# Four tokens to a partition, one factor for the first batch, and a tail that is planned backwards

## The chip, the cores and the metric

The kernel runs on one core of one Trainium2 chip. The metric is the device time in microseconds from start to end of one launch. A core has five engines that run side by side, each in the order of its own instructions: TensorE (PE, matrix products), VectorE (DVE), ScalarE (ACT), GpSimd (POOL) and SyncE (SP, here only an issuer of transfers). Each waits on semaphores for what it needs of the others.

## The reference

Four layers of a graph network over 32 batches of 512 tokens with 128 features; `adj` is one 512 x 512 matrix for all. Each layer adds its result to x.

```python
h = relu(layernorm(x));  x = x + L0(h, adj)       # GCN
h = relu(layernorm(x));  x = x + L1(h, adj)       # gated graph network, 5 steps
h = relu(layernorm(x));  x = x + L2(h, adj)       # graph attention, softmax over neighbours, elu
h = relu(layernorm(x));  x = x + L3(h, adj)       # graph attention without elu

# L0
A = adj + I;  d = A.sum(-1) ** -0.5
out = (d[:, None] * A * d[None, :]) @ h @ W.T + b
# L1, five times (in_matrix and out_matrix are both adj)
m = adj @ h
z = sigmoid([m, m] @ w3.T + h @ u3.T + ...);  r = sigmoid([m, m] @ w4.T + h @ u3.T + ...)
hv = tanh([m, m] @ w5.T + (r * h) @ u5.T + ...);  h = (1 - z) * h + z * hv
# L2, L3
g = h @ W;  e = leaky_relu(g @ a_src + (g @ a_dst).T), only where there is an edge
out = softmax(e) @ g
```

## The kernel before

The kernel doesn't write its instructions in program order. It collects operations, each with an engine, an estimated cost, a due time and what it reads and writes. Then a planner simulates the engines with those costs and emits the instructions in the order that it found. The buffers are pools: a value takes a free one when its first operation starts, and gives it back after the last.

```python
class Plan:
    def run(self):
        for o in reversed(self.ops):
            o.tail = o.cost + o.delay + max((q.tail for q in o.then), default=0)
        ...
        best = min(self.ends, key=lambda end: self.attempt(uses, *end))
        self.attempt(uses, *best)
        for o in self.order:
            o.emit()

    def attempt(self, uses, last, hurry):
        for o in self.ops:
            o.soon = min(o.due, last - o.tail * hurry)     # the priority of an operation
        # ... list scheduling: of the ready operations of an engine for which buffers
        #     are free, the one with the smallest o.soon starts

# pools (cut):  8 PSUM banks, 13 x, 2 "e" (scores, [128, 4, 512] f32), 4 "off", ...
# 16 pairs (last, hurry) are tried
```

Loads. Token c * 128 + p lies on partition p, so a partition gets four pieces of 512 bytes of x; of adj it gets one row of 2 KB per piece c.

```python
nc.sync.dma_start(v.t, x[b].rearrange("(c p) d -> p c d", p=P))              # L259, each batch
q.dma_start(adj_sb.t[:, c, :], adj[c * P:(c + 1) * P, :])                    # L264, on ACT and SP in turn
w0 = load("w0", ...)                                                         # L237, then b0, w4, w3, w5, u3, u5
```

The start. adj is turned on TensorE (L295), its degrees are summed (two pieces on ScalarE, two on VectorE, L303), and one power on GpSimd makes `dinv` (L306). Batch 0 is normalized on VectorE with its own power `rstd` (L402), and then multiplied by `dinv`. Its product with adj takes adj + I on the diagonal blocks (`diag`, L314).

```python
op("POOL", 1.0, ..., pow(deg, -0.5) -> dinv)                                 # L306
for m in range(C):
    op("DVE", 0.16, ..., diag[m] = block(adjT, m) + ident)                   # L314
...
norm(b, y, -802)                     # bn_stats, bn_aggr, pow on POOL (L402), (x - mean) * rstd (L423)
op("DVE", 0.16, ..., y = max(y, 0) * dinv)                                   # L596, four times

def product(h, due):                                                         # L559
    for c in range(C):
        for lo, hi in ((0, c), (c, c + 1), (c + 1, C)):
            if lo < hi:
                right = diag.t[:, c, :] if lo == c else adjT.t[:, c, lo * P:hi * P]
                nc.tensor.matmul(..., h.t[:, c, :], right, ...)
```

The GCN of the later batches and the steps of the gated network form their products with adj by seven half products for a pair of batches (L520), of which four take prepared sums of adj's quarters ("made"). There are two such sets, one of adj and one of the normalized adj ("an").

The tail. The attention of the last four batches ("near") takes the path through TensorE in place of transfers: centre and relu on VectorE, turn, heads, score rows spread by TensorE, scores on VectorE, and a mix that starts with each score block.

```python
def center_relu(b, y, due):
    for c in range(C):
        op("DVE", 0.21, ..., bn_stats(st[c], x[c]))                          # L431
        op("DVE", 0.07, ..., bn_aggr(mv[c], st[c]))                          # L432
        op("DVE", 0.16, ..., y[c] = max(x[c] - mean[c], 0))                  # L433
    op("DVE", 0.1, ..., ve = var + EPS)                                      # L436
    op("POOL", 1.0, ..., rstd = ve ** -0.5)                                  # L437

# gat, near:  turn y (L452), copy (L730), heads (L743), exp of three columns (L748),
#   factor g (L751), scale (L756), spread the row (L772), then for each block j:
#   e[j] = max(row, column) * mask             on VectorE, 128 x 512         # L785
#   four products of e[j] with h               on TensorE, 128 x 129         # L794
#   reciprocal (L808), then L2: v (L810), exp (L824), sums (L825, L827);  L3: x += p * rden (L816), output (L838)
# the other batches: mix at L805, gates of the gated network at L653, L654, L660, L667, L668
```

Of the kernel before, what the change touches and what calls it, by code (L numbers as in the profile page):

```python
# [15 lines left out]
P = 128  # L16
# [7 lines left out]
FAR0, FAR1 = 2, 4  # L24
RUN_UP = 8
# [14 lines left out]
class Op:  # L40
    def __init__(self, engine, cost, due, emit, delay):
        self.engine, self.cost, self.due, self.emit, self.delay = engine, cost, due, emit, delay
        self.waits, self.then, self.vals = 0, [], []


class Plan:
# [5 lines left out]
    def __init__(self, buffers, ends):  # L52
        self.buffers, self.ends, self.ops = buffers, ends, []

# [28 lines left out]

    def run(self):

        for o in reversed(self.ops):
            o.tail = o.cost + o.delay + max((q.tail for q in o.then), default=0)
            o.first = o.waits
        uses = {v: v.uses for o in self.ops for v in o.vals}
        best = min(self.ends, key=lambda end: self.attempt(uses, *end))  # L90
        self.attempt(uses, *best)
        assert self.end < math.inf, "the order has come to a stop"
        for o in self.order:
            o.emit()

    def attempt(self, uses, last, hurry):
        for v, n in uses.items():
            v.uses = n
            if v.kind:
                v.t = None  # L100
        for o in self.ops:
            o.waits = o.first

            o.soon = min(o.due, last - o.tail * hurry)
# [7 lines left out]
        now, count = 0.0, 0  # L112
# [6 lines left out]
        def start(e):  # L119
            if busy[e]:  # L120
                return
            kept = []
            while ready[e]:
                key = heapq.heappop(ready[e])
                o = self.ops[key[1]]
                opens = [v for v in o.vals if v.kind and v.t is None]
                short = [v for v in opens if len(free[v.kind]) < sum(u.kind == v.kind for u in opens)]
                if not short:
                    for v in opens:
                        v.t = free[v.kind].pop()  # L130
                    busy[e] = True
                    o.at = now
                    order.append(o)
                    post(now + o.cost, 0, o)
                    post(now + o.cost + o.delay, 1, o)
                    break
                kept.append(key)
            for key in kept:
                heapq.heappush(ready[e], key)

# [9 lines left out]
        while events:  # L150
            now, _, kind, o = heapq.heappop(events)
            if kind == 0:
                busy[o.engine] = False
                settle(o, True)
            else:
                done += 1
                settle(o, False)
                for v in o.vals:
                    v.uses -= 1
                    if not v.uses and v.kind:  # L160
                        free[v.kind].append(v.t)
            for e in ready:
                start(e)
# [5 lines left out]
def gnn_stack(ctx: ExitStack, tc: tile.TileContext, a: dict, out: bass.AP):  # L169
# [3 lines left out]
    C = N // P  # L173

# [8 lines left out]
    def flat(t):  # L183
# [25 lines left out]
        "e": tiles(2, [P, C, N], "e"),  # L209
# [6 lines left out]
        "off": tiles(4, SMALL, "off"),  # L216
        "rden": tiles(3, SMALL, "rden"),
    }, [(last, hurry) for last in (170, 173, 176, 179) for hurry in (0.06, 0.08, 0.1, 0.12)])
# [15 lines left out]
    def load(name, shape, src, due, queue="SP", cost=0.45, delay=3.6):  # L234
        v = fixed(shape, name)
        q = {"SP": nc.sync, "POOL": nc.gpsimd, "AQ": nc.scalar}[queue]
        op(queue if queue != "AQ" else "ACT", cost, due, lambda: q.dma_start(v.t, src), w=[v], delay=delay)  # L237
        return v
# [17 lines left out]
    for b in range(B):  # L256
        v = Val("x", C)
        op("SP", 0.5, -1002 if b == 0 else max(-995 + b, STEPS * b - 20) if b >= 8 else -995 + b,
           lambda v=v, b=b: nc.sync.dma_start(v.t, x[b].rearrange("(c p) d -> p c d", p=P)), w=[v], delay=3.5 if b == 0 else 3 if b > 3 else 4)  # L259
        xs.append(v)  # L260
    adj_sb = Val("e", C)
    for c in range(C):
        e, q = (("ACT", nc.scalar), ("SP", nc.sync))[c % 2]
        op(e, 0.45, -1001, lambda c=c, q=q: q.dma_start(adj_sb.t[:, c, :], adj[c * P:(c + 1) * P, :]),  # L264
           w=[adj_sb[c]], delay=3 if c == 0 else 4.2)
    w0 = load("w0", [P, D], a["L0_gnn_W"], -994.5)
# [4 lines left out]
    for k in ("w4", "w3", "w5", "u3", "u5"):  # L271
        src = a[f"L1_gnn_{k}_w"]
        raw[k] = load(k, [P, src.shape[1]], src, -993.3)
# [15 lines left out]
    for c in range(C):  # L289
# [3 lines left out]
        def turn_adj(c=c, p=p):  # L293
            for m in range(C):
                nc.tensor.transpose(p.t[:, m, :], adj_sb.t[:, c, m * P:(m + 1) * P], ident.t)  # L295
        op("PE", C * TURN, -800, turn_adj, r=[adj_sb[c], ident], w=[p])
        op("ACT", A, -800, lambda c=c, p=p: nc.scalar.copy(adjT.t[:, :, c * P:(c + 1) * P], p.t), r=[p], w=[adjT[c]])
        if c < 2:
# [3 lines left out]
        else:  # L302
            op("DVE", 0.66, -801, lambda c=c: nc.vector.reduce_sum(deg.t[:, c:c + 1], adj_sb.t[:, c, :], axis=mybir.AxisListType.X),  # L303
               r=[adj_sb[c]], w=[deg[c]])
    op("DVE", 0.1, -801, lambda: nc.vector.tensor_scalar_add(deg.t, deg.t, 1.0), w=[deg])
    op("POOL", 1.0, -1000, lambda: nc.gpsimd.tensor_tensor(dinv.t, deg.t, mhalf.t, ALU.pow), r=[deg, mhalf], w=[dinv])  # L306

# [5 lines left out]
    for m in range(C):  # L313
        op("DVE", 0.16, -799.5, lambda m=m: nc.vector.tensor_add(diag.t[:, m, :], block(adjT.t, m), ident.t),  # L314
           r=[adjT[m], ident], w=[diag[m]])

    def right_factors(mT, due):


        made = fixed([P, 4, 2, 2 * P], "made", 4)  # L320
# [4 lines left out]
        f |= {k: (lambda i=i: made.t[:, i], made[i]) for i, k in enumerate((2, 1, 4, 6))}  # L325
# [20 lines left out]
    def transposed(due, *group, then=()):  # L346

        p = Val("bank", len(group))
        t = fixed([P, len(group), P], "wT")
        for i, (parts, _) in enumerate(group):  # L350
# [3 lines left out]
            op("PE", len(parts) * MM1, due, turns, r=[ident, minus, *then] + [q[0] for q in parts], w=[p[i]])  # L354
# [13 lines left out]
    w0T = transposed(-750, (one(w0), 1), then=turned)  # L368
    gates = transposed(-700, (halves("w4"), 1), (one(raw["u3"]), 1), (halves("w3") + halves("w4", minus), 1), (halves("w5"), 1), then=turned)
    u5T = transposed(-690, (one(raw["u5"]), 0.5), then=turned)  # L370
# [21 lines left out]
    def norm_stats(b, due):  # L392
        xb, st, mv, ve, rstd = xs[b], Val("st", C), Val("mv"), Val("ve"), Val("rstd")
# [8 lines left out]
        op("POOL", 1.0, due, lambda: nc.gpsimd.tensor_tensor(rstd.t, ve.t, mhalf.t, ALU.pow), r=[ve, mhalf], w=[rstd])  # L402
        return mv, rstd

    def norm_relu(b, y, due, times=None):

        xb, off = xs[b], Val("off")
        mv, rstd = norm_stats(b, due)
# [9 lines left out]
    def norm(b, y, due):  # L418

        xb = xs[b]  # L420
        mv, rstd = norm_stats(b, due)
        for c in range(C):
            op("DVE", 0.16, due, lambda c=c: nc.vector.tensor_scalar(  # L423
                y.t[:, c, :], xb.t[:, c, :], mv.t[:, c, 0:1], rstd.t[:, c:c + 1], op0=ALU.subtract, op1=ALU.mult),
               r=[xb[c], mv, rstd], w=[y[c]])

    def center_relu(b, y, due):

        xb, st, mv, ve, rstd = xs[b], Val("st", C), Val("mv", C), Val("ve"), Val("rstd")
        for c in range(C):  # L430
            op("DVE", 0.21, due, lambda c=c: nc.vector.bn_stats(st.t[:, c, :], xb.t[:, c, :]), r=[xb[c]], w=[st[c]])  # L431
            op("DVE", 0.07, due, lambda c=c: nc.vector.bn_aggr(mv.t[:, c, :], st.t[:, c, :]), r=[st[c]], w=[mv[c]])  # L432
            op("DVE", 0.16, due, lambda c=c: nc.vector.tensor_scalar(  # L433
                y.t[:, c, :], xb.t[:, c, :], mv.t[:, c, 0:1], 0.0, op0=ALU.subtract, op1=ALU.max),
               r=[xb[c], mv[c]], w=[y[c]])
# [115 lines left out]
    def product(h, due):  # L551

        p, m = Val("bank"), Val("m")
        for c in range(C):
            def times(c=c):
                for lo, hi in ((0, c), (c, c + 1), (c + 1, C)):
                    if lo < hi:
                        right = diag.t[:, c, :] if lo == c else adjT.t[:, c, lo * P:hi * P]
                        nc.tensor.matmul(flat(p.t)[:, lo * P:hi * P], h.t[:, c, :], right, start=c == lo == 0, stop=c == C - 1,  # L559
                                         skip_group_check=True)  # L560
            op("PE", MM, due, times, r=[h[c], adjT[c], diag[c]], w=[p, m])
# [3 lines left out]
    def normalized(begun):  # L565
# [18 lines left out]
        return anT, right_factors(anT, 0)  # L584
# [4 lines left out]
    def gcn(pair, due):  # L589
        first, ys = pair[0] < 4, []  # L590
        for i, b in enumerate(pair):
            y = Val("y", C) if first else Val("pair", 2)
            if b == 0:
                norm(b, y, -802)
                for c in range(C):
                    op("DVE", 0.16, -800, lambda c=c, y=y: nc.vector.tensor_scalar(  # L596
                        y.t[:, c, :], y.t[:, c, :], 0.0, dinv.t[:, c:c + 1], op0=ALU.max, op1=ALU.mult), r=[dinv], w=[y[c]])
            else:
                norm_relu(b, y, -798 if b == 1 else due + i, dinv if first else None)
# [4 lines left out]
        ms = [product(y, due + i) for i, y in enumerate(ys)] if first else products(*ys, factors["an"], due + 1)  # L604
# [117 lines left out]
    def gat(b, l, due):  # L722
# [113 lines left out]
        elif near:  # L836
            for a in range(2):
                op("SP", 0.45, due + 4, lambda a=a: nc.sync.dma_start(  # L838
                    out[b].rearrange("(c p) d -> p c d", p=P)[:, 2 * a:2 * a + 2], xb.t[:, 2 * a:2 * a + 2]),
                   r=[xb[2 * a], xb[2 * a + 1]])  # L840
        else:
            op("SP", 0.95, due + 4, lambda: nc.sync.dma_start(out[b].rearrange("(c p) d -> p c d", p=P), xb.t), r=[xb])
# [63 lines left out]
```

## Time and profile before

| what | value |
|---|---|
| time, median of 3 runs | 1633.63 us (1631.4 to 1633.82) |
| span of the profiled run | 1631.2 us |
| mean granted TensorE clock | 0.999 |
| TensorE, VectorE, ScalarE, GpSimd busy | 99%, 85%, 44%, 9% |
| transfers | 374176 packets, 157.72 MB, 38.5% of 16 engines' time in the main queue |

How to read it: a matrix product of 32-bit floats shows as two records[...]; a turn by the transpose instruction shows as one. The records of TensorE overlap, so a mean duration is longer than the distance from one start to the next, and the pieces of the chain of waits give the better rate. A row of the timeline has the start, the length, the engine, the line, the operation, the tiles and, in brackets, how long the engine was idle before it and what released it.

### The profile page before, as it was taken

To read this page: it belongs to the slowest core of one execution; us is meant where nothing else is said; L and a number is where in the kernel's file an instruction comes from. 1 tells how busy PE (TensorE), PEld (TensorE's weight loads), DVE (VectorE), ACT (ScalarE), POOL (GpSimd) and SP (SyncE) were. 2 spreads that over 40 slices of the span, in tenths; PEclk is the share of its full clock that TensorE was granted. 3 is DMA by queue.
4 is the path that set the end of the run, shared out by engine and by line. 5 is a ranking of instruction groups with operands and counts; after the bars stand their busy time and mean duration, and the time that the engine had idled before them with its cause. 6 is when DMAs were issued, how large, how long until landed. Compare 5 with 4: busy or idle time off the path is not lost.

```text
span 1631.2 us, 23929 instructions
## 1 busy us (share of the span) xinstructions
PE 1617.3 (99%) x7330; PEld 1169.2 (72%) x7330; DVE 1386.3 (85%) x3989; ACT 716.1 (44%) x1593; POOL 143.2 (9%) x136
## 2 busy tenths in 40 slices
PE   9999999999999999999999999999999999999998
PEld 7666666776776777777776766767677777676777
DVE  8968688898978898888898888888887888777888
ACT  5653443535335344444535345353443533434343
POOL 2200000010001100000111001110000000000001
PEclk9999999999999999999999999999999999999999
DMA  4134353534436344353433535344362323434010
GB/s 130 33 71 104 81 120 91 124 98 106 115 82 147 82 117 104 91 135 84 121 101 96 137 79 134 88 106 118 82 146 73 98 72 84 123 91 110 27 40 27
DMA packets 374176, 157.72 MB, mean 97 GB/s; under 512 B 201664, under 2 KB 355616, under 8 KB 374048
## 3 DMA queue, kind: packets, MB, share of 16 engines
q1 hardware_dynamic: 373760, 155.67, 38.5%
q8 instruction: 58, 0.95, 0.2%
q14 instruction: 70, 0.57, 0.1%
q10 hardware_dynamic: 288, 0.52, 0.1%
HBM read 86.25 MB, written 69.84 MB: 96 GB/s over the span
## 4 chain that ended last, share of the span: by engine, by line
PE 95%; DVE 3%; ACT 1%; DMA 0%; POOL 0%; issue 0%; DVEq 0%; POOLq 0%; ACTq 0%
PE bank L520 35%; PE bank L805 12%; PE bank L653 8%; PE bank L654 8%; PE bank L667 8%; PE bank L660 8%; PE bank L668 8%; PE bank L743 3%; PE bank L612 2%; PE bank L559 1%; PE bank L794 1%; DVE e L785 1%; PE bank L452 1%; POOL rstd L402 0%; DMA w<-in_L_gnn_w_w_dram 0%
## 5 line engine op out<-in xcount | busy, mean ns | idle before, releaser
L520 PE MATMUL bank<-made,S 128*128 128x256 f32 x1128 | 269.5, 380 | 1.2 <-ACT half L525 0.9
L402 POOL TENSOR_TENSOR rstd<-ve,mhalf 128x4 f32<-128x4 f32 x120 | 132.8, 1108 | 1397.5 <-DVE ve L400 1130.6
L520 PEld LDWEIGHTS bank<-made,S 128*128 128x128 f32 x1128 | 217.2, 196 | 40.4 <-issue 17.2
L525 ACT COPY half<-bank 128x256 f32<-128x256 f32 x282 | 104.4, 370 | 258.7 <-PE bank L520 255.7
L805 PEld LDWEIGHTS bank<-h_gat,e 128*128 128x128 f32 x1792 | 207.9, 192 | 13.0 <-issue 11.2
L805 PE MATMUL bank<-h_gat,e 128*128 128x129 f32 x1792 | 208.6, 275 | 0.0
L656 ACT ACTIVATE r<-bank,gate_bw 128x512 f32<-128x512 f32 x160 | 109.6, 685 | 213.5 <-PE bank L654 190.2
L672 DVE TENSOR_TENSOR hv<-hv,hT 128x512 f32<-128x512 f32 x160 | 109.3, 683 | 85.3 <-ACT hv L670 84.9
L658 DVE SCALAR_TENSOR_TENSOR rh<-r,hT 128x512 f32<-128x512 f32 x160 | 110.0, 687 | 67.4 <-ACT r L656 66.5
L653 PE MATMUL bank<-m,wT 128*128 128x512 f32 x320 | 163.7, 593 | 0.0
L667 PE MATMUL bank<-m,wT 128*128 128x512 f32 x320 | 163.4, 592 | 0.0
L654 PE MATMUL bank<-hT,wT 128*128 128x512 f32 x320 | 163.4, 592 | 0.0
L668 PE MATMUL bank<-rh,wT 128*128 128x512 f32 x320 | 163.4, 592 | 0.0
L660 PE MATMUL bank<-m,wT 128*128 128x512 f32 x320 | 163.3, 592 | 0.0
L670 ACT ACTIVATE hv<-bank,gate_bw 128x512 f32<-128x512 f32 x160 | 109.5, 684 | 118.9 <-PE bank L668 117.6
L785 DVE SCALAR_TENSOR_TENSOR e<-row,h_gat,maskT 128x512 f32<-128x512 f32 x224 | 161.4, 740 | 0.0
L520 PE MATMUL bank<-adjT,h 128*128 128x256 f32 x640 | 159.5, 380 | 0.5 <-ACT h L687 0.5
L520 PEld LDWEIGHTS bank<-adjT,h 128*128 128x128 f32 x640 | 123.3, 196 | 25.2 <-issue 13.4
L533 DVE TENSOR_TENSOR m<-half,bank 128x256 f32<-128x256 f32 x282 | 115.9, 412 | 24.3 <-ACT half L525 12.0
L662 ACT ACTIVATE z<-bank,gate_bw 128x512 f32<-128x512 f32 x160 | 109.6, 685 | 51.5 <-PE bank L660 49.8
L395 DVE BATCH_NORM_STATS2 st<-x 128x6 f32<-128x128 f32 x480 | 115.4, 279 | 4.7 <-DMA x<-in_x_dram 4.4
L654 PEld LDWEIGHTS bank<-hT,wT 128*128 128x128 f32 x320 | 60.8, 190 | 76.5 <-issue 75.1
(137 smaller groups left out, 2278.8 us busy)
## 6 DMA issues: line engine op xcount, KB each, us to landing
far<-sq SPq DMA_DIRECT2D x920, 64.0 KB
h<-far SPq DMA_DIRECT2D x240, 128.0 KB
gT<-far SPq DMA_DIRECT2D x56, 256.0 KB
row<-line SPq DMA_DIRECT2D x56, 256.0 KB
x<-in_x_dram SPq DMA_DIRECT2D x32, 256.0 KB
h<-far SPq DMA_DIRECT2D x28, 256.0 KB
out_dram<-x SPq DMA_DIRECT2D x28, 256.0 KB
hT<-far SPq DMA_DIRECT2D x104, 64.0 KB
```

Source lines behind the costliest of these rows:

```text
L395: op("DVE", 0.21, due, lambda c=c: nc.vector.bn_stats(st.t[:, c, :], xb.t[:, c, :]), r=[xb[c]], w=[st[c]])
L402: op("POOL", 1.0, due, lambda: nc.gpsimd.tensor_tensor(rstd.t, ve.t, mhalf.t, ALU.pow), r=[ve, mhalf], w=[rstd])
L520: nc.tensor.matmul(low(r), u[:, l, :], factors[k][0]()[:, l, :], start=fresh and l == 0, stop=l == 1, skip_group_check=not fresh)
L533: op("DVE", HV, due - 5, lambda: nc.vector.tensor_add(out(), u.t, low(t)), r=[u, t], w=[o])
L653: nc.tensor.matmul(flat(gate.t), gates.t[:, 0, :], flat(m.t), start=True, stop=False)
L654: nc.tensor.matmul(flat(gate.t), gates.t[:, 1, :], flat(hT.t), start=False, stop=True)
L658: op("DVE", V, due - 5, lambda: nc.vector.scalar_tensor_tensor(flat(rh.t), flat(r.t), 1.0, flat(hT.t), op0=ALU.add, op1=ALU.mult), r=[r, h ...
L660: op("PE", MM, due + 0.3, lambda: nc.tensor.matmul(flat(gate.t), gates.t[:, 2, :], flat(m.t), start=False, stop=True, skip_group_check=Tru ...
L667: nc.tensor.matmul(flat(cand.t), gates.t[:, 3, :], flat(m.t), start=True, stop=False)
L668: nc.tensor.matmul(flat(cand.t), u5T.t[:, 0, :], flat(rh.t), start=False, stop=True)
L785: op("DVE", 0.68, due + 3, lambda j=j: nc.vector.scalar_tensor_tensor(e.t[:, j, :], rows(row.t), h.t[:, j, D + 1:D + 2], mask(j), op0=ALU. ...
L805: nc.tensor.matmul(pt()[:, c, :D + 1], e.t[:, j, i * P:(i + 1) * P], h.t[:, j, :D + 1], start=(j == 0), stop=(j == C - 1))
```

## The change

- Layout: token p * 4 + c lies on partition p, so a partition's part of x and of the result is one piece of 2 KB (1 KB for the outputs of the last four batches, which go in two halves). adj is loaded and turned in the same order of tokens.
- Batch 0: relu(x - mean) is multiplied by one factor ((deg + 1)(var + eps)) ** -0.5, whose power is taken in two pieces (three columns, then one). Its product adds h times the identity instead of reading `diag`. Weights are loaded in another order, and some are turned later.
- The last four batches: the relu after centring moves from VectorE to ScalarE.
- A third score buffer "e"; the second set of made factors is kept in one of the three until the last GCN pair is done.
- The planner: it starts from three pairs (last, hurry), and from each goes up to five times through the plan backwards, from the end, to find how late each operation may start; operations after 1350 us of the plan take that as their priority. After 1420 us it may put an idle transpose on TensorE where 0.9 us of the last 3.4 would be without work.
- Estimated delays of the first loads are set anew.

The diff, shortened: "..." marks cuts, and some bodies are told in a line.

```diff
-        best = min(self.ends, key=lambda end: self.attempt(uses, *end))
-        self.attempt(uses, *best)
+        for last, hurry in self.ends:
+            for again in range(6):
+                if again:
+                    late = self.put_off()
+                for o in self.ops:
+                    if not again:
+                        o.soon = min(o.due, last - o.tail * hurry)
+                    else:
+                        o.soon = late[o] / self.SLOT if o.at > self.near_end else o.due
+                self.attempt()
+    def put_off(self):
+        # list scheduling from the end: an operation is ready when all that need it are placed,
+        # and of the ready ones that which ended last in the plan so far comes first
...
+            if e == "PE" and left and not busy[e] and now > self.idle_from and free["bank"]:
+                keep_going()
...
-        "e": tiles(2, [P, C, N], "e"),
+        "e": tiles(3, [P, C, N], "e"),
-        "off": tiles(4, SMALL, "off"),
+        "off": tiles(6, SMALL, "off"),
-    }, [(last, hurry) for last in (170, 173, 176, 179) for hurry in (0.06, 0.08, 0.1, 0.12)])
+    }, [(179, 0.06), (175, 0.06), (177, 0.12)], 1350,
+        IDLE_FROM, lambda v: nc.tensor.transpose(v.t[:, 0, :], ident.t, ident.t))
...
-           lambda v=v, b=b: nc.sync.dma_start(v.t, x[b].rearrange("(c p) d -> p c d", p=P)), ...)
+           lambda v=v, b=b: nc.sync.dma_start(v.t, x[b].rearrange("(p c) d -> p c d", c=C)), ...)
-        op(e, 0.45, -1001, lambda c=c, q=q: q.dma_start(adj_sb.t[:, c, :], adj[c * P:(c + 1) * P, :]), ...)
+        op(e, 0.45, -1001, lambda c=c, q=q: q.dma_start(adj_sb.t[:, c, :], adj.rearrange("(p c) n -> c p n", c=C)[c]), ...)
-                nc.tensor.transpose(p.t[:, m, :], adj_sb.t[:, c, m * P:(m + 1) * P], ident.t)
+                nc.tensor.transpose(p.t[:, m, :], adj_sb.t[:, c].rearrange("p (n m) -> p m n", m=C)[:, m], ident.t)
...
-        made = fixed([P, 4, 2, 2 * P], "made", 4)
+        made = Val("e", 4) if passing else fixed([P, C, N], "made", 4)      # passing for "an"
...
-    w0T = transposed(-750, (one(w0), 1), then=turned)
+    w0T = transposed(-9.2, (one(w0), 1), then=turned)
+    # of the gates' weights u3 and w5 are due at -9.5, w4 and w3 stay at -700; u5 at -9.4
...
+    def norm_first(b, y):
+        for parts in ((0, 2, 1), (3,)):
+            op("DVE", 0.8, ..., deg of the last part;  f = (deg + 1) * ve)
+            op("POOL", 1.0, ..., f = f ** -0.5)
+            op("DVE", 0.1, ..., off = -mean * f)
+        op("DVE", 0.2, ..., y[0] = max(x[0] - mean, 0));  op("DVE", 0.2, ..., y[0] *= f[0])
+        for c in range(1, C):
+            op("ACT", 0.385, ..., y[c] = relu(f[c] * x[c] + off[c]))
...
     def center_relu(b, y, due):
-            op("DVE", 0.16, ..., y[c] = max(x[c] - mean[c], 0))
+        for a in range(2):
+            op("DVE", 0.22, ..., bn_aggr of two pieces, off = -mean)
+            op("ACT", 0.385, ..., y[c] = relu(x[c] + off[c]))               # twice
...
     def product(h, due, by_diag):
+                if by_diag:
+                    terms = [(0, c, row[:, :c * P]), (c, c + 1, diag.t[:, c, :]), (c + 1, C, row[:, (c + 1) * P:])]
+                else:
+                    terms = [(0, C, row), (c, c + 1, ident.t)]              # batch 0
...
-                    out[b].rearrange("(c p) d -> p c d", p=P)[:, 2 * a:2 * a + 2], ...)
+                    out[b].rearrange("(p c) d -> p c d", c=C)[:, 2 * a:2 * a + 2], ...)
```

## The prediction

> **What bounds the kernel now.** I read the page first (busy time and the chain that ended last), then the windows by stage, and then the timeline of the first 12 us and the chain of the last 50 us. From the page:
>
> ```profile
> span 1631.2 us, 23929 instructions
> PE 1617.3 (99%) x7330; PEld 1169.2 (72%) x7330; DVE 1386.3 (85%) x3989; ACT 716.1 (44%) x1593; POOL 143.2 (9%) x136
> ...
> PE 95%; DVE 3%; ACT 1%; DMA 0%; POOL 0%; issue 0%; DVEq 0%; POOLq 0%; ACTq 0%
> ```
>
> TensorE is busy 99% of the span and is 95% of the chain. The change removes no product, so its whole field is the time in which TensorE does not work at its rate. How much is that? Busy time overlaps and flatters, so I use start-to-start times from the chain: 0.429 us for a record of 512 columns ("0.86 PE bank L653 x2"), 0.2165 for 256 ("3.46 PE bank L520 x16"), 0.1117 for 129 or 131, 0.11 for 128. Counts from the groups: 2632 x 0.2165 = 570, 1600 x 0.429 = 686, 2048 x 0.1117 = 229, 512 x 0.1117 = 57, the rest about 63. Sum 1605 us, the warm-up at the start left out. The span less the 4.35 us until the first piece of adj has landed, and less the 5.3 us behind the last product (last sums on VectorE and the output's landing), is 1621.5. So about 16.5 us are lost, 1% of the span, and a change of this kind cannot reach 2% (32 us). Where they lie (windows; columns: stretch, its length, then busy time and count of PE, PEld, DVE, ACT, POOL, then clock, DMA share, GB/s):
>
> ```profile
> 0.00:10.00 10.00, 7.75 (x44) 7.13 (x45) 5.03 (x24) 5.33 (x12) 2.86 (x9) 1.00 0.84 250
> ...
> 400.00:800.00 400.00, 399.51 (x1781) 287.00 (x1781) 348.24 (x997) 178.22 (x390) 36.76 (x33) 1.00 0.43 107
> ...
> 1580.00:1600.00 20.00, 19.43 (x167) 18.69 (x166) 19.34 (x76) 9.00 (x32) 2.47 (x3) 1.00 0.05 14
> 1600.00:1610.00 10.00, 9.57 (x82) 8.94 (x81) 10.00 (x35) 3.92 (x12) 1.53 (x2) 1.00 0.01 2
> 1610.00:1620.00 10.00, 7.96 (x56) 7.49 (x55) 8.74 (x36) 4.09 (x17) 1.01 (x1) 0.83 0.09 26
> 1620.00:1631.20 11.20, 6.77 (x61) 6.58 (x59) 6.40 (x21) 0.69 (x3) 0.00 (x0) 1.00 0.25 72
> ```
>
> The middle is full. The tail is not, and there VectorE is at 97 to 100% while ScalarE is at 40 to 45%; from 1610 the clock falls to 0.83. The chain of the tail shows the same:
>
> ```profile
> 1612.79 0.20 DVE off L751 x3
> 1613.00 1.33 DVE e L785 x2
> 1614.33 0.04 issue
> 1614.38 1.12 PE bank L772 x4
> 1615.49 2.80 PE bank L794 x16
> ...
> 1620.51 5.38 PE bank L794 x48
> ```
>
> The chain runs on VectorE nearly without a break from 1585.2 to 1614.3. After that TensorE is slow: 16 records in 2.80 us and 4 in 1.12, where the row of 48 gives 0.112 each (1.79 and 0.44). That is 1.7 us lost to the clock alone. The start, from the timeline:
>
> ```profile
> 6.03 1.69 PE L295 MATMUL bank<-ident,e 128*128 128x128 f32 x12 [0.35 <-DMA e<-in_adj_dram]
> 7.56 0.39 PE L353 MATMUL bank<-ident,w 128*128 128x128 f32 x2
> 8.79 1.16 PE L353 MATMUL bank<-ident,w 128*128 128x128 f32 x8 [0.84 <-DMA w<-in_L_gnn_w_w_dram]
> 8.91 1.59 POOL L306 TENSOR_TENSOR dinv<-deg,mhalf 128x4 f32<-128x4 f32 x1 [1.39 <-DVE deg L305]
> 10.54 0.88 DVE L596 TENSOR_SCALAR y<-y,dinv 128x128 f32<-128x128 f32 x4 [0.31 <-POOL dinv L306]
> 11.13 0.39 PE L559 MATMUL bank<-v,y 128*128 128x128 f32 x2
> ```
>
> The first product waits for two powers on GpSimd in a row (rstd, then dinv); TensorE fills the time with turned weights and waits for those too.
>
> **What the Trainium skill says.** "TensorE: Matmul & The Clock Gate", section "What's actually happening": the clock is passed or halved by how busy TensorE was in a window of about 3.4 us. The trace agrees in kind: the slow records come after waits of 0.40 us at 1609.6 and 1.93 us at 1613.6. "VectorE: DVE Perf Modes", section on the TRN2 errata: each operation from SBUF pays a fixed time beside its elements, on VectorE and ScalarE. The trace agrees: a 128x512 score takes 742 ns and a 128x128 centring still 276 alone (about 195 back to back). So moving a small operation from one engine to the other moves its whole fixed cost. "DMA: Bandwidth & Descriptors", section "Why small descriptors are slow (HBM only)": a fixed cost per packet. In this trace the queues stand at 300 to 400 GB/s from 3 to 10 us, with 512-byte and 2 KB packets mixed; how much the 512-byte ones cost there no row tells.
>
> **The change part by part.**
>
> *Layout.* An x load goes from 512 packets of 512 bytes to 128 of 2 KB, an output alike (1 KB in the last four batches). adj's rows were 2 KB before. All 32 loads and outputs but the first four lie under the full middle: worth 0 there. Only the start can feel it, where x0, x1 and 1 MB of adj share the queues.
>
> *Batch 0 by one factor.* Relu commutes with the positive factor, so rstd and dinv become one power of (deg+1)(var+eps). From the instruction order of the changed kernel with the durations above: adj is all turned at 7.6 as before; VectorE has the stats of x0 by 6.35, one centring and one sum of degrees by about 7.3; GpSimd's power of three columns (1.0 to 1.1 us) ends at about 8.6; the first y is ready at about 8.8, against 10.8. Product 0 now has 4 x (512 + 128) columns in two passes, 4 x 1.08 = 4.3 us against 3.5, since it adds the identity instead of waiting for the diagonal sums. Before it TensorE turns only 12 weight records (w4 and w3, now loaded earlier, so the wait of 0.84 goes); the other 10 (1.1 us) come after. So y1 is wanted at 8.9 + 4.3 + 1.1 = 14.3 us, against 14.76 before, with the same work done. Gain about 0.4 us; 2.3 us earlier in the first product is mostly paid back in the longer product and the weights that move behind it.
>
> *Relu of the last four batches on ScalarE.* Per attention 4 centrings (4 x 0.195) leave VectorE and 2 small negations (2 x 0.075) come: 0.6 us less, eight times. ScalarE has room (45% busy). It costs latency: four relus at about 0.39 instead of 0.2.
>
> *Third score buffer.* It is the place of the second set of made factors, which ends with the last GCN pair; so it is free exactly for the tail, and two attentions need no longer wait for each other's e.
>
> *Planned backwards.* The order is what matters. In the old order 40.1 us of TensorE work (counted, at the rates above) lie behind the last gate product, which ends at 1579.9; the last product ends at 1625.9. So 46.0 us for 40.1: 5.9 lost. In the new order 46.4 us of work lie behind it (28 + 108 + 44 + 24 + 32 instructions there against 24 + 112 + 16 + 24 + 32): attention products of earlier batches are held back as filling. VectorE's work behind the last new state is 39.2 us against 37.5, with a head of some 4 us before it: 43, against 46.4 + 2.5 for TensorE and the last sums. So VectorE has 5.7 us of slack where it had none (37.5 with a head of 5 from 1579.9 to 1585, 42.5 against 42.6). No filler product (the idle transpose) was placed at all, so the plan sees no 3.4 us stretch with 0.9 us of idling after 1420. I estimate 1.5 of the 5.9 us remain: 4.4 gained, the clock's 1.7 within it. From 1400 to 1580 about 3.6 us are lost before; I let the change win 1.5.
>
> Sum: 0.4 + 4.4 + 1.5 = 6.3 us. 1633.6 - 6.3 = 1627.3, said as 1627.5.
>
> **The rivals.** First, everything fits: the tail keeps no loss, the wider packets bring x0 in half a microsecond earlier. For it: the counted slack on VectorE. That is 5.9 + 3 + 1.5, about 10 us, 1623. Second, the new order is right only by the plan's own costs, and each engine runs in order: a late small operation stops TensorE. For it: powers on GpSimd took 1.0 to 1.6 us in the trace where the plan writes 1.0, and VectorE runs attentions of four batches interleaved with little between them; relus on ScalarE make the last batch's chain longer by about 0.8 us in each of two attentions. That would give back 3 to 5 us: 1630 to 1632. Third, the change of priorities moves the middle too (the order differs nearly from the first row), and a shuttle through memory then lands late. For it: seven waits of TensorE for a copied half product, 3.2 us in all. Against it: DMA share 0.43 and nothing of the middle's chain on DMA. It could cost 2 to 6 us: up to 1634.
>
> **Range and chances.** The gain has a ceiling of about 12 us (16.5 less what a start and an end always cost) and a floor a little above zero if the second or third rival holds. I take 1622 to 1632.5. A change by 2% either way is outside anything the trace offers.
>
> **What would show it.** Start: the first batch-0 product near 8.9 us and batch 1's near 14.3. Tail: the chain on TensorE, not VectorE, from the last gate on; clock 1.00 in every window; TensorE behind the last gate losing under 2 us; the stretch from there to the end about as long as before (some 51 us) while the last gate comes 4 to 6 us earlier. Wrong it would be if VectorE still ended the waits of the tail, if the clock still fell, or if the middle lost what the tail won.

## The result, and the profile after

| | before | after |
|---|---|---|
| time, median | 1633.57 us (6 runs, 1631.4 to 1633.82) | 1624.25 us (6 runs, 1623.91 to 1625.03) |
| ratio after / before | | 0.9946, 95% interval 0.9933 to 0.9959 |
| span of the profiled run | 1631.2 us | 1623.2 us |
| packets | 374176 | 350113 |

The change takes 9.3 us off the median; by the ratio in the table that is 0.54%. The page of the changed kernel, its top and its chain:

```profile
span 1623.2 us, 24004 instructions
PE 1614.7 (99%) x7326; PEld 1169.0 (72%) x7326; DVE 1378.4 (85%) x3971; ACT 724.6 (45%) x1628; POOL 146.1 (9%) x137
...
PE 94%; DVE 3%; DMA 1%; ACT 0%; POOL 0%; issue 0%; SPq 0%; DVEq 0%; ACTq 0%; POOLq 0%
```

The top of the page hardly moved: TensorE had 99% and has 99%. The gain can only be seen by stage. The windows of the changed kernel (columns as in the table of before: PE, PEld, DVE, ACT, POOL with counts, clock, DMA share, GB/s):

```profile
0.00:10.00 10.00, 7.78 (x36) 7.12 (x37) 4.21 (x22) 4.93 (x11) 2.41 (x10) 1.00 0.69 223
...
400.00:800.00 400.00, 400.00 (x1796) 288.85 (x1795) 348.01 (x993) 174.81 (x387) 34.75 (x31) 1.00 0.43 107
...
1450.00:1500.00 50.00, 50.00 (x234) 35.88 (x233) 41.33 (x108) 21.01 (x46) 2.36 (x3) 1.00 0.43 106
...
1580.00:1600.00 20.00, 20.00 (x180) 19.87 (x179) 19.79 (x71) 11.27 (x43) 2.01 (x2) 1.00 0.13 48
1600.00:1610.00 10.00, 9.46 (x85) 9.27 (x84) 9.70 (x45) 5.75 (x20) 2.01 (x2) 1.00 0.04 14
1610.00:1623.20 13.20, 9.28 (x82) 8.92 (x80) 9.11 (x28) 2.71 (x11) 0.00 (x0) 1.00 0.24 81
```

From 1400 to 1600 TensorE now has no gap (in the kernel before it was busy 48.80 of the 50 us from 1450 to 1500), and the clock stays at 1.00 to the end. VectorE is as busy in the tail as before (19.79 of 20), but it no longer sets the pace: ahead of the last sums it has one stretch of 5.7 us left in the chain, from 1601.9 to 1607.6.

```profile
1598.13 3.57 PE bank L905 x32
1601.70 0.23 PE bank L883 x2
1601.94 0.01 issue
1601.95 0.17 DVE rden L919
...
1606.92 0.66 DVE e L896
1607.59 0.04 issue
1607.63 1.16 PE bank L905 x8
...
1613.96 5.38 PE bank L905 x48
1619.33 0.02 issue
1619.36 0.17 DVE rden L919
...
1620.03 0.52 DVE x L927 x2
```

The start went the other way. Timeline of the start (start, length, engine, line, operation, count, idle before); L342 is the warm-up, products of zeros that only keep TensorE busy until adj is there:

```profile
1.05 3.78 PE L342 MATMUL bank<-hv 128*128 128x128 f32 x16 [1.05 <-DVE hv L335]
...
5.53 0.63 ACT L390 ACTIVATE r<-e 128x512 f32<-128x512 f32 x1 [2.18 <-DMA e<-in_adj_dram]
...
5.65 1.10 PE L385 MATMUL bank<-ident,e 128*128 128x128 f32 x4 [0.81 <-DMA e<-in_adj_dram]
7.10 2.72 PE L385 MATMUL bank<-ident,e 128*128 128x128 f32 x12 [0.35 <-DMA e<-in_adj_dram]
9.66 1.06 PE L440 MATMUL bank<-ident,w 128*128 128x128 f32 x8
10.55 0.61 PE L440 MATMUL bank<-minus,w 128*128 128x128 f32 x4
11.00 1.02 PE L673 MATMUL bank<-adjT,y 128*128 128x512 f32 x2
```

adj's first piece landed at 5.53 us (4.36 before; here and below this is when ScalarE's first sum of it starts), and the 12 turns after it took 2.56 us from their first start to the next operation (1.53 before). So the first product came at 11.00 us, no earlier than before (11.13).

A ledger of the 8.0 us between the two spans. I count TensorE's records in a stretch and price them at their start-to-start rates, as in the prediction; a stretch's length less that is its loss.

| part | before | after | gain |
|---|---|---|---|
| TensorE work still to do at 1400 us | 216.1 | 217.4 (0.8 of the difference is the longer product of batch 0) | -1.3 |
| loss from 1400 to the end of the last gate product (1579.87; 1571.46) | 3.9 | 0.4 | 3.5 |
| loss from there to the end of TensorE's last product (1626.77; 1619.32) | 6.8 | 1.5 | 5.3 |
| from TensorE's last product to the end of the span | 4.4 | 3.9 | 0.5 |

The last two rows of the kernel before are not those of the prediction, which took 1625.9 for the end of its last product. That is where the chain leaves TensorE (5.38 us from 1620.51); eight more records of the last product follow, as the timeline shows:

```profile
1620.35 6.42 PE L794 MATMUL bank<-h_gat,e 128*128 128x129 f32 x56
...
1626.00 1.11 DVE L816 SCALAR_TENSOR_TENSOR x<-bank,rden,x 128x128 f32<-128x128 f32 x4
...
1627.22 1.13 DVE L816 SCALAR_TENSOR_TENSOR x<-bank,rden,x 128x128 f32<-128x128 f32 x4
```

### The profile page after: what moved, and what is told of

The parts are those of the page before. It is cut to its first block, busy times and chain, and to the rows that moved or that the text cites. A ratio compares the mean times of both kernels' runs of the same rounds, so it can differ in the third digit from the quotient of the medians.

```text
span 1623.2 us, 24004 instructions
## 1 busy us (share of the span) xinstructions
PE 1614.7 (99%) x7326; PEld 1169.0 (72%) x7326; DVE 1378.4 (85%) x3971; ACT 724.6 (45%) x1628; POOL 146.1 (9%) x137
## 2 busy tenths in 40 slices
DMA packets 350113, 157.72 MB, mean 97 GB/s; under 512 B 201664, under 2 KB 323872, under 8 KB 349984
## 4 chain that ended last, share of the span: by engine, by line
PE 94%; DVE 3%; DMA 1%; ACT 0%; POOL 0%; issue 0%; SPq 0%; DVEq 0%; ACTq 0%; POOLq 0%
PE bank L630 33%; PE bank L916 12%; PE bank L764 8%; PE bank L765 8%; PE bank L778 8%; PE bank L771 8%; PE bank L779 8%; PE bank L854 3%; PE bank L723 2%; PE bank L905 2%; PE bank L673 1%; PE bank L562 1%; DMA e<-in_adj_dram 0%; DVE st L482 0%; POOL rstd L495 0%
## 5 line engine op out<-in xcount | busy, mean ns | idle before, releaser
L630 PE MATMUL bank<-made,S 128*128 128x256 f32 x960 | 230.6, 380 | 0.5 <-DVE m L643 0.3
L916 PE MATMUL bank<-h_gat,e 128*128 128x129 f32 x1792 | 212.3, 275 | 0.0
L630 PEld LDWEIGHTS bank<-made,S 128*128 128x128 f32 x960 | 184.2, 196 | 31.3 <-issue 12.5
L779 PEld LDWEIGHTS bank<-rh,wT 128*128 128x128 f32 x320 | 60.8, 190 | 76.5 <-issue 66.3
```

Source lines behind the costliest of these rows:

```text
L630: nc.tensor.matmul(low(r), u[:, l, :], factors[k][0]()[:, l, :], start=fresh and l == 0, stop=l == 1, skip_group_check=not fresh)
L779: nc.tensor.matmul(flat(cand.t), u5T.t[:, 0, :], flat(rh.t), start=False, stop=True)
L916: nc.tensor.matmul(pt()[:, c, :D + 1], e.t[:, j, i * P:(i + 1) * P], h.t[:, j, :D + 1], start=(j == 0), stop=(j == C - 1))
```

## The experiments

Each was timed in five rounds, where nothing else is said, beside the kernel before. The control, the changed kernel once more beside the second group:

> The changed kernel once more, beside the next three on the same chip, as what they are measured against: 1624.3 within 1 us.

Measured: 1624.04 us (1623.3 to 1625.28), ratio 0.9951 (0.9938 to 0.9963). The kernel before took 1632.69 there.

### The layout

**e1: the changed kernel with the old layout.** Its order of instructions is the same.

```diff
-x[b].rearrange("(p c) d -> p c d", c=C)            # loads, and out[b] alike
+x[b].rearrange("(c p) d -> p c d", p=P)
-adj.rearrange("(p c) n -> c p n", c=C)[c]
+adj[c * P:(c + 1) * P, :]
-adj_sb.t[:, c].rearrange("p (n m) -> p m n", m=C)[:, m]
+adj_sb.t[:, c, m * P:(m + 1) * P]
```

> The changed kernel with the old layout of x, adj and the result (512-byte packets, adj rows of a block in sequence, turned without a stride), in the same order of instructions. Theory A (the new layout is what made the start late: adj landed 1.15 us later and was turned at twice the cost): adj is turned by about 8 us instead of 9.8, the first product of batch 0 comes at about 9.5 instead of 11.0, and the end comes 0.3 to 1.5 us earlier, 1623 to 1624. Rival (the wide packets pay in the middle or at the end, where outputs and shuttles share the queues): 1626 or more. If the start's delay is absorbed before 40 us, where VectorE is busy without a break, the time stays at 1624.3 within 0.5.

Measured: 1623.34 us (1623.1 to 1625.45), ratio 0.9947 (0.9935 to 0.996). Timeline of TensorE:

```profile
4.63 2.86 PE L385 MATMUL bank<-ident,e 128*128 128x128 f32 x16
7.32 1.06 PE L440 MATMUL bank<-ident,w 128*128 128x128 f32 x8
8.22 0.61 PE L440 MATMUL bank<-minus,w 128*128 128x128 f32 x4
8.95 1.10 PE L673 MATMUL bank<-adjT,y 128*128 128x512 f32 x2
...
14.47 0.39 PE L673 MATMUL bank<-v,y 128*128 128x128 f32 x2
```

With the old layout the start is what the prediction had for the changed kernel: first product at 8.95 us (8.9 foreseen), batch 1's at 14.47 (14.3). The time lies in Theory A's range. By 20 us TensorE had done 14.0 us of work against 12.0 in the changed kernel's profile, and at 1400 it was still 2.1 ahead: the span is 1621.3 (1623.2). So a microsecond at the start is not absorbed later. But these two profiles are of the quickest of e1's five runs and of the slowest of the changed kernel's six; against the profile of the control (span 1622.3) e1 is 1.1 ahead at 1400.

**e1 again**, on the chip of the control, beside e10, e11 and e8:

> The changed kernel with the old layout once more: the best so far, to see whether it is the best by more than chance. Theory A: 0.5 to 1.5 us below the changed kernel, 1622.8 to 1623.8, adj landing before 5.1 us. Rival: its first time was luck of the start, and it comes to 1624 to 1624.5.

Measured: 1623.37 us (1622.95 to 1624.07), ratio 0.9947 (0.9934 to 0.9959), adj's first piece at 4.95 us. Again Theory A's range was met. Both times the median is 0.7 to 0.9 us under the changed kernel's two, but the intervals of the ratios overlap: it has the lowest medians of all versions, and that it is faster than the changed kernel is not shown.

**e2: the kernel before with the new layout**, in its own order.

> The kernel before with the new layout alone, in its old order. Theory A: the start comes 1 to 2 us later and the end 0.5 to 1.5 us later, 1634 to 1635. Rival (the layout is worth something by itself): 1632 or less.

Measured: 1632.33 us, ratio 1.0001 (0.9993 to 1.001), between the two ranges. adj came late here too (turned from 5.75 us on), but the old batch 0 waits for the second power on GpSimd anyway, and its first product moved only from 11.13 to 11.49. The new layout by itself, with 24,000 packets fewer and adj later, is worth nothing that shows.

**e8: x in the new layout, adj in the old one.** One run of it was timed; it leaves out the right pairing of adj's tokens with x's.

> The changed kernel with adj loaded and turned in the old order of rows, x and the result in the new one. It leaves out the right pairing of adj's tokens with x's; the work is the same. If the wide packets of x hold adj up, its first piece lands at 5.3 us or later, as in the changed kernel; if adj's row distance of 8 KB does, it lands before 4.6.

Measured: adj's first piece at 5.13 us, between the two marks. In the nine profiles with both in the new layout it landed at 5.2 to 5.8 us, in the four with both in the old one at 3.9 to 5.0. So the layout delays adj by about 1 us in the mean, with much chance in each run; whether x's packets or adj's row distance does it is not settled.

### The clock at the start

**e10: a longer warm-up.**

```diff
-for _ in range(RUN_UP):
+for _ in range(RUN_UP + 4):
```

> The changed kernel with 12 warm-up products in place of 8, in the same order otherwise. In the profiles so far adj landed at 5.3 to 5.95 us with the new layout, after the warm-up had ended at 4.8, and in some of them the 12 turns that follow took about 0.21 us each in place of 0.13. Theory F (TensorE's pause before adj lets the clock fall; the warm-up bridges it): the turns take 0.13 us or less each, the first product of batch 0 comes by 10.2 us, and the time is 0.3 to 1 us less, 1623.3 to 1624. Rival (the turns are slow by their stride, or by chance that the warm-up doesn't touch): 1624.2 within 0.5, with slow turns seen again.

Measured: 1623.78 us, and all five between 1623.67 and 1623.92; ratio 0.9949 (0.9936 to 0.9961). The times of Theory F came: the first product at 10.11 us, the last 12 turns in 1.55 us, and no slow turns in its profile. The control's five runs spread over 2.0 us, these over 0.25. The median is 0.3 to 0.5 us lower, and this is not shown to be more than noise, since the intervals overlap.

The mechanism that Theory F named is, in most profiles, not what happened. The control's profile:

```profile
1.05 3.78 PE L342 MATMUL bank<-hv 128*128 128x128 f32 x16 [1.05 <-DVE hv L335]
5.95 0.72 PE L385 MATMUL bank<-ident,e 128*128 128x128 f32 x4 [1.12 <-DMA e<-in_adj_dram]
7.09 1.71 PE L385 MATMUL bank<-ident,e 128*128 128x128 f32 x12 [0.42 <-DMA e<-in_adj_dram]
8.64 1.06 PE L440 MATMUL bank<-ident,w 128*128 128x128 f32 x8
```

Here the last 12 turns took 1.55 us, 0.13 each; in the profile shown first, with the same instructions, 2.56 us, 0.21 each. So the stride in the turned operand (which both have) isn't the cause. But in both profiles the 16 records of the warm-up already stand 0.21 us apart, twice the 0.11 of the weights that are turned later: the array was not at full rate when the pause began. What differs is when it got there. The stored trace keeps records of the granted clock, which no view lists; the first of them, at 1.00, is at 5.07 us in the control and at 9.57 in the profile shown first, and the distance of TensorE's records halves at that point, or behind the pause that it falls in, in each of the fourteen profiles. Four of the five with slow turns (the changed kernel, and of the runs below e3b, e5 and e11) had not had the full clock before, since their first record is at 9.57 to 10.53. Only e3 had it and lost it: 1.00 from 3.89, 0.50 from 7.30, 1.00 from 10.72, in steps of 3.41 us.

"TensorE: Matmul & The Clock Gate", section "What's actually happening", says that the clock follows a window of about 3.4 us that runs free of the kernel's start, so that the same kernel differs from run to run. That agrees, and the fourteen profiles show how full a window had to be: the 3.41 us ahead of the first full clock hold at most 0.74 us without work on TensorE, each stretch of 3.41 us before that at least 0.92 (1.06 in the profile shown first, where the pause before adj lies in it). So the pause does not pull the clock down as a rule; it keeps it from rising, for one window more. In e10 there is no pause, and its first clock record is at 6.58:

```profile
1.05 5.49 PE L342 MATMUL bank<-hv 128*128 128x128 f32 x24 [1.05 <-DVE hv L335]
6.33 2.39 PE L385 MATMUL bank<-ident,e 128*128 128x128 f32 x16
```

It has a price: adj had landed at 5.66 us, and its turns waited for the end of the warm-up. The clock column of the windows needs care here. Where the trace has no clock record yet, it shows 1.00. Windows of the changed kernel (first record at 9.57), then of e3 (below), both with slow turns:

```profile
8.00:9.00 1.00, 1.00 (x7) 1.00 (x6) 0.94 (x5) 0.59 (x1) 0.66 (x1) 1.00 0.78 236
```

```profile
8.00:9.00 1.00, 1.00 (x6) 1.00 (x5) 0.96 (x5) 0.73 (x2) 0.91 (x2) 0.50 0.78 248
```

At the start the count of records per microsecond (7 and 6 here, 11 in the control) tells more than this column.

### The plan

**e3: the old planner with everything else changed**, without idle transposes.

```diff
-[(179, 0.06), (175, 0.06), (177, 0.12)]
+[(last, hurry) for last in (170, 173, 176, 179) for hurry in (0.06, 0.08, 0.1, 0.12)]
-for again in range(6):
+for again in range(1):
-IDLE_FROM = 1420
+IDLE_FROM = 1e9
```

> The changed kernel with the old planner: forward only, with the 16 old pairs, no idle transposes; layout, batch 0, relu on ScalarE and third score buffer as changed. Theory B (the backward plan is the main gain, since it is what holds attention products back as filling): 1629 to 1632, and behind the last gate TensorE again loses 4 us or more. Rival (VectorE's relief and the third buffer make the gain, any order will do): 1624 to 1626.

Measured: 1639.85 us (1639.25 to 1641.51), ratio 1.0047 (1.0034 to 1.0059). The theory had the sign and not the size: this is 15.8 us slower than the control and 7 slower than the kernel before. Windows:

```profile
1450.00:1500.00 50.00, 47.03 (x200) 31.38 (x199) 39.46 (x107) 20.41 (x43) 3.71 (x3) 1.00 0.39 98
...
1610.00:1620.00 10.00, 7.42 (x36) 5.56 (x34) 8.64 (x39) 6.48 (x22) 1.98 (x2) 0.75 0.00 0
```

TensorE waits at 1450 to 1500 already, and its last gate product ends at 1584.8, 13 us after the changed kernel's. Behind it lie 38.3 us of its work, done in 48.6: the forward order keeps less back as filling and loses 10.2 us there (6.8 in the kernel before).

**e3b: the same with the idle transposes** (59 of them in the order).

> As the one before, with the idle transposes where the forward plan has them (56). Theory C (in the old tail the fallen clock cost by itself, 1.7 us in the profile of the kernel before): 1 to 2 us faster than without, and no stretch with a clock under 1. Rival (the waits set the end, the clock only shows them): within 0.5 us of the one without, or slower, since the transposes stand in front of work that has become ready.

Measured: 1637.42 us (1636.31 to 1637.83), ratio 1.0029 (1.0018 to 1.004): 2.4 us faster in the median. By the work done, 0.4 of the 1.9 us between the spans was there by 100 us, before any idle transpose; some 1.5 is the tail's. Its window:

```profile
1610.00:1620.00 10.00, 8.88 (x71) 7.83 (x70) 8.40 (x38) 7.30 (x26) 1.98 (x2) 1.00 0.01 2
```

The clock is 1.00 where it was 0.75. So a fallen clock does cost by itself: some 1.5 us here, where e3's clock records stand at 0.50 for 6.8 us from 1614.98 on. The prediction read off 1.7 us for the kernel before, whose records stand at 0.50 for 3.4 us from 1614.06 on. The changed kernel's order holds no idle transpose, and its clock stays at 1.00 without them.

**e9: the backward plan alone.** Layout, batch 0, relu on VectorE and two score buffers are as before; the order of the first loads and the later turning of weights stay.

```diff
-"e": tiles(3, [P, C, N], "e"),   right_factors(anT, 0, True)
+"e": tiles(2, [P, C, N], "e"),   right_factors(anT, 0)
-def norm_first / center_relu / the layouts of the change
+those of the kernel before
```

> The backward plan alone: the planner, its three starting pairs, the loading order and the later turning of some weights stay as changed; layout, batch 0, relu on VectorE and two score buffers with a fixed second set of made factors are as before. The forward plan with all the rest was 7 us slower than the kernel before, so the order must carry more than the whole gain. Theory B (the backward order is enough by itself): 1624 to 1628. Rival (the backward order gains only because the third buffer and the relief of VectorE give it room): 1630 or more.

Measured: 1630.93 us (1630.47 to 1632.0), ratio 0.9992 (0.9984 to 1.0). The rival is right: of the 8.7 us to the control the plan alone brings 1.8, and hardly clear of nothing. Its last gate product ends at 1571.0, as early as the changed kernel's, with 51.2 us of work behind it (4.4 of them idle transposes), done in 54.3. But then it is VectorE again that sets the pace in places, and the last two attentions end together. Windows and the end of its chain:

```profile
1580.00:1600.00 20.00, 19.30 (x170) 18.66 (x169) 18.47 (x73) 7.95 (x29) 3.14 (x3) 1.00 0.20 57
1600.00:1610.00 10.00, 9.62 (x86) 9.07 (x84) 9.85 (x38) 3.64 (x11) 0.00 (x0) 1.00 0.04 13
```

```profile
1607.42 1.42 PE bank L308 x13
...
1619.07 5.38 PE bank L892 x48
...
1626.38 0.52 DVE x L914 x2
```

L308 are idle transposes: 13 in a row are 1.4 us with nothing to do. e9 also lacks the new start: its first product comes at 10.66 us.

**e4: two score buffers**, with a fixed second set of made factors, planned anew.

```diff
-"e": tiles(3, [P, C, N], "e"),   right_factors(anT, 0, True)
+"e": tiles(2, [P, C, N], "e"),   right_factors(anT, 0)
```

> The changed kernel with two score buffers and a fixed second set of made factors, planned anew by the same backward planner. Theory D (the third buffer lets a third attention's scores stand ready as filling): 1626 to 1628, with idle of TensorE behind a score in the tail. Rival (two are enough once the order is right): 1624 to 1625.

Measured: 1628.71 us (1626.91 to 1628.94), ratio 0.9975 (0.9965 to 0.9985), 4.7 us over the control: Theory D, and more than it had. The profile caught the quickest of its eight runs (1626.91), so that it shows only 2.8 of the 4.7 us. Who kept TensorE waiting (line waited for: us in total, times, longest), and a window:

```profile
PE bank L905 <- DVE e L896: 1.0, 3, 0.6
...
PE bank L562 <- DVE v L921: 0.8, 1, 0.8
```

```profile
1600.00:1610.00 10.00, 8.94 (x78) 8.53 (x78) 9.86 (x46) 5.56 (x20) 1.01 (x1) 1.00 0.00 1
```

Mixes wait for scores and turns for the softmax's quotient; in the changed kernel such waits are 0.5 us in all.

**e5: relu of the last four batches on VectorE**, planned anew.

```diff
-op("ACT", 0.385, ..., y[c] = relu(x[c] + off[c]))
+op("DVE", 0.16, ..., y[c] = max(x[c] - mean[c], 0))
```

> The changed kernel with the relu of the last four batches back on VectorE (about 0.6 us more VectorE work in each of eight attentions), planned anew by the same planner. Theory E (VectorE's relief is part of the gain, though the counted slack behind the last gate is 5.7 us against some 3 us that come back there): 1625 to 1627. Rival (slack takes it all, and the shorter chain of the last batch even gains): 1623.5 to 1624.5.

Measured: 1628.61 us (1627.48 to 1629.11), ratio 0.9975 (0.9966 to 0.9984), 4.6 us over the control, above Theory E's range. The counted slack did not take it:

```profile
1580.00:1600.00 20.00, 19.20 (x171) 18.99 (x171) 19.87 (x67) 7.88 (x29) 2.01 (x2) 1.00 0.14 48
```

VectorE is full, TensorE loses 0.8 us in this window, and from where the chain leaves TensorE to the end 5.4 us pass again (5.3 before, 3.9 in the changed kernel).

**e11: other starting pairs for the planner**, to see how much of such differences is the luck of a plan.

```diff
-[(179, 0.06), (175, 0.06), (177, 0.12)]
+[(176, 0.08), (173, 0.1), (170, 0.12)]
```

> The changed kernel with other starting pairs for the planner, (176, 0.08), (173, 0.1), (170, 0.12), in place of (179, 0.06), (175, 0.06), (177, 0.12): how far a plan's luck goes. If the losses of the runs with two score buffers and with relu on VectorE (4 to 5 us each) are real, this stays within 2 us of 1624. Rival (any new plan costs some 4 us, since the pairs were picked for this kernel): 1627 or more.

Measured: 1625.16 us (1623.79 to 1625.79), ratio 0.9957 (0.9943 to 0.997), 1.1 over the control, in ranges that overlap; its profile is one with slow turns. So 4 to 5 us are more than the one other plan that was tried costs; a wider sample of plans was not taken. Parts of the change were left out one at a time and once all together; their sum (4.7 and 4.6 of 8.7) is not to be read as a budget, since what each of plan, buffer and relief brings depends on the others.

## Why the prediction was right

It said 1627.5 (1622 to 1632.5) and no change by 2%; measured were 1624.25 and a ratio of 0.9946. The gain was 9.3 us and not 6.1. By its steps, set beside the 8.0 us of the ledger:

- **The ceiling.** TensorE bound, some 17 us of loss in all, 2% out of reach: right. No version here comes below 1622.9.
- **Behind the last gate product, 4.4 us**: right in its reason, and too small by 0.9: 5.3. The step was read short, as said at the ledger: 46.9 us passed there for 40.1 of work, so 6.8 were lost and not 5.9. For the new order 46.4 us of work were foreseen with 1.5 lost, and that is what came: 47.9 us from 1571.46 to 1619.32. VectorE lost its place in the chain but for 5.7 us, and the clock held. e4 and e5 show that both pieces of relief are needed.
- **The slack of VectorE, 5.7 us**: wrong. From the last new state to VectorE's last sum (1574.8 to 1620.6) it is busy 43.7 of 45.8 us, where the prediction had summed 39.2 of work. This slack made e5's rival look likely; and a sum of work over 40 us doesn't tell that the work is there in time.
- **From 1400 to 1580, 1.5 us**: mis-sized. The loss fell from 3.9 to 0.4 us, so 3.5.
- **The end, taken as equal**: 4.4 us became 3.9. In the old order the last two attentions ended together, with eight sums of VectorE behind them from 1626.0 on; in the new one the one before last is done earlier. Counted from where the chain leaves TensorE the end went from 5.3 to 3.9 us, and in e9, in which they end together again, it is 5.2.
- **The start, a gain of 0.4 us**: failed in the changed kernel, which at 1400 has 1.3 us more left to do. The step that failed was "adj is all turned at 7.6 as before": in the profile it was turned at 9.7, with adj landing 1.2 us later and the clock granted only at 9.57. In the control, with the clock granted in time, it was turned at 8.6, and 0.4 us more were left at 1400. For the layout the prediction had a small gain at most, and no loss. The factor itself does what was worked out: 8.95 and 14.47 us in e1. The two powers of the kernel before, though, did not stand in a row: in the prediction's own line of L306 GpSimd was idle for 1.39 us, waiting for VectorE's sum of degrees.
- **The rivals.** The second (late small operations give 3 to 5 us back) and the third (the middle loses) did not come: of the work done, the changed kernel is 0.5 us behind by 100 us and still 0.5 by 1400. The first, all fits, 1623, was nearer than the stated middle.

So the mechanism of the tail was right, and that the number came as near as it did owes something to luck: the start fell short by 1.7 us, and the other three terms brought 3.4 more than foreseen.

A remark on the spans: the profiled run of the changed kernel was one with slow turns (1625.03 us), which is part of why the spans differ by 8.0 and the medians by 9.3.

## What to carry to other kernels

When one engine is busy 99%, price its records at their start-to-start rate and list the loss by stage: that gives the ceiling of a change before it is made, and the ledger after it. Work held back as filling for a tail needs an engine that feeds it in time, and a buffer to run ahead: here the whole change brought 8.7 us and the order alone 1.8. A start that is late stays late to the end in a kernel with one full engine, so look at what a new layout does to the very first transfers, and see from the distance of TensorE's records whether the warm-up has brought the clock up by the time they land.

## What was not expected of the hardware

- Two runs of the same instructions differ by 1 us at the start: 12 turns in 1.55 or in 2.56 us, by whether the full clock was granted at 5.07 or at 9.57 us. A warm-up of 3.8 us did not settle it: over the thirteen profiles with eight warm-up products the full clock came first at 3.89 to 10.53 us. Four more products took the spread of five runs from 2.0 to 0.25 us.
- In all fourteen profiles the clock first rose at the end of 3.41 us in which TensorE was without work for 0.74 us or less, and not where it was 0.92 us or more.
- The windows' clock column said 1.00 in one run in which those turns were slow, and 0.50 in another. Both are true to the trace: the first had no clock record before 9.57 us.
- Loading the turned operand with a stride of 16 bytes lengthens its load (0.21 us against 0.14 a record) and hardly the distance of the turns (0.12 us against 0.11 at full clock).
- adj's first piece, issued at 0.73 or 0.74 us each time, landed anywhere from 3.9 to 5.0 us with the old layout and from 5.2 to 5.8 with the new one. Why is open.

## What stays open

Why the forward plan with everything else changed is 7 us slower than the kernel before was not taken apart: by the ledger 1.7 of the 6.8 us between the spans are the start's, 1.4 lie between 1400 and the last gate (where 3 us of 1450 to 1500 are idle) and 3.4 behind it, but which choice of the plan made them is not seen. Whether the wide packets or the row distance delay adj was not settled. The old layout and the longer warm-up were not tried together.
